# Matmuls without a use in TensorE's waits of the ramp, and seven of batch 1's last fills loaded ahead

## Chip, cores and metric

The kernel runs on one core of a Trainium2 chip. The metric is the device time of the launch in microseconds; the profile's times are microseconds from the first instruction of the program.

## The reference, cut to what matters

```python
xn = layernorm(x)                                    # x: 2 batches x 1024 rows x 1024
s  = xn @ (W * blockmask).T + bias                   # mask of 32x32 blocks
q  = xn.mean(rows) @ Wq.T                            # one query per batch
coeffs = softmax(q @ keys.T / sqrt(128))             # 8 experts, per batch
g  = silu(xn @ W_org.T + sum_e coeffs[e] * (xn @ down[e]) @ up[e])
out = x + s * g
```

So there are two products of 1024 x 1024 x 1024 for each batch: one with the masked weight (called "s" in the kernel), and one with a weight that is W_org plus the experts' low-rank parts, mixed per batch (called "y"). Then they are multiplied, and x is added.

## The kernel before, in words

**Precision by splitting.** Each factor of a product is split in a high part (a cast to the matmul's fp32r type, done on ScalarE) and a low part (the rest, a subtraction on VectorE). A product is three matmuls for each slice of the inner dimension: high by high, high by low, low by high. In `open_gemm` these are lines 441 to 443; its inner function `part(k0, k1)` issues them for slices k0 to k1.

**The ramp.** The first 60 us are ordered by hand on TensorE, VectorE, ScalarE and GpSimd (`manual_schedule`): these engines follow the written order. Row blocks of x are loaded, normalised and transposed on TensorE (`x_turn`, L200), cast and subtracted out of PSUM (`x_hi` L588, `x_lo` L592), while the mask is summed by blocks (`mask_sum`), spread by eight small matmuls (`mask_apply_mm`, L265) and multiplied into the weight (`w_mul`, L571), which is cast (`w_hi`, L576) and subtracted (`w_lo`, L580). `t0` and `t1` are the `part` functions of the first two output tiles in PSUM, p0 and p1: with the first 256 columns of the weight. `warm_up(n)` (L661) issues n matmuls of 128x512 with ones, whose result nobody reads. They run 13 times at the start (`NWARM`), 8 times after row block 0's transposes (`NWARM2`), twice after the mask's matmuls and four times ahead of t0. The parts that the prediction follows stand in the code in this order: `t0(0, 2)`, `w_lo(0, 2)`, `t0(2, 4)`, `x_hi(1, 0)`, `x_lo(1, 0)`, ..., `t1(0, 2)`, `x_turn(1, 1)`, `t1(2, 4)`, `x_lo(0, 1)`, `x_hi(1, 1)`, statistics of row block 2, a mask sum on ScalarE, `t0(4, 8)`, `x_lo(1, 1)`, `shift_of(2)`, the two halves of row block 2's norm, `t1(4, 7)`, `x_turn(2, 0)`, and so on.

**Batch 0** is then computed tile by tile. Meanwhile VectorE prepares sums and differences of batch 1's normalised input and stores them to memory (`xv`).

**Batch 1** uses a scheme of seven products instead of eight for a block of two by two (`quad`): a unit is one pair of 128 output columns for one of the two weights; it has seven factors of the weight, in `raw` (rows of 4 x 128 values in a partition: rows 0 to 3 are loaded, `unit_sum` makes sums in rows 4 to 6 and in row 2), which `unit_split` (L1082 cast, L1083 subtraction) turns into high and low in the tile `ow`. The seven factors of x are loaded from `xv` by `fill` (L1038 load, L1039 cast, L1040 subtraction) into four tiles `xw[j]`, each with seven pieces m. A fill's load goes through a staging buffer, `xs_pool`, with four buffers. The tiles xw[2] and xw[3] take the places of batch 0's x and of batch 0's masked weight, so their casts can't begin before the last tile of batch 0, `s_tile(7)`, has been computed. `product(u, a, m, ...)` (L1190) multiplies factor a of the weight by piece m.

In `quad`, `after(k)` runs the k-th list of `behind`, and `slot(k)` the k-th list of `ahead`, the preparation of the next unit. For unit 0 `behind` holds fills. The products' order is (0, 0) into pa, (4, 3) into py, (5, 4) into pb, (1, 1) into pa, (2, 5) into pb, (6, 2) into py, (3, 6) into pa. Between them ScalarE copies pa into pb (L1221), takes the snapshots s5 of py and s2 of pb (`snap`, L1197), evacuates pa (`out_tile`) and copies pb into pa (L1251); each copy is ahead of the next product that adds to the same place.

**The last tile of batch 0** is evacuated by `flush()` (VectorE L458 and L488), x is added to it by an accumulating transfer of GpSimd (L491), and it is stored by GpSimd (L506). Only then are the pools of batch 0 closed (`late_cms`), in whose place unit 1's `ow` is opened.

Outside of the ramp a scheduler places the instructions, with the written order as its priority; in the trace VectorE and ScalarE follow the written order.

Of the kernel before, what the change touches and what calls it, by code (L numbers as in the profile page):

```python
# [25 lines left out]
E_, R_, KQ = 8, 64, 128  # L26
EPS = 1e-5
NWARM = 13
NWARM2 = 8


@with_exitstack
def kernel(
# [94 lines left out]
    raw = natp.tile([P, 7, 4, P], F32, name="raw")  # L128
# [142 lines left out]
    def mask_apply_cp(qr):  # L271
        nc.vector.tensor_copy(m_sb[:, :, 8 * qr : 8 * (qr + 1)], spread[qr])
# [158 lines left out]
    def open_gemm(b, i, w, c0=0, n=NH):  # L431

        ps = ps_acc.tile([P, NH], F32, name="acc_ps", tag="acc_ps")[:, :n]
        g, j = divmod(i, 4)
        xs = xg[(b, g)]
        cols = slice(j * P, (j + 1) * P)
        wc = slice(c0, c0 + n)

        def part(k0, k1):
            for kt in range(k0, k1):  # L440
                nc.tensor.matmul(ps, lhsT=xs[:, kt, 0, cols], rhs=w[:, kt, 0, wc], start=kt == 0, stop=False)  # L441
                nc.tensor.matmul(ps, lhsT=xs[:, kt, 0, cols], rhs=w[:, kt, 1, wc], start=False, stop=False)  # L442
                nc.tensor.matmul(ps, lhsT=xs[:, kt, 1, cols], rhs=w[:, kt, 0, wc], start=False, stop=kt == NKT - 1)  # L443

        return ps, part
# [94 lines left out]
    J = lambda f, *a: (lambda: f(*a))  # L540
# [43 lines left out]
    def x_turn(i, h):  # L584
        turn((i, h), lambda k: xr[i][:, (4 * h + k) * P : (4 * h + k + 1) * P])

    def x_hi(i, h):
        nc.scalar.copy(g0[:, 4 * h : 4 * h + 4, 0, i * P : (i + 1) * P], turned[(i, h)])  # L588
# [7 lines left out]
    def x_stats(i, h):  # L596
        bn(i, xr[i], h)
# [41 lines left out]
    with tc.manual_schedule(engines={mybir.EngineType.PE, mybir.EngineType.DVE, mybir.EngineType.Activation, mybir.EngineType.Pool}):  # L639
# [19 lines left out]
        def warm_up(n):  # L659
            for _ in range(n):  # L660
                nc.tensor.matmul(  # L661
                    warm, lhsT=ones_r, rhs=ones_r.unsqueeze(1).to_broadcast([P, 4, P]), start=True, stop=True
                )
# [9 lines left out]
        x_turn(0, 1)  # L673
        warm_up(NWARM2)
        x_stats(1, 0)
# [7 lines left out]
        mask_spread(0)  # L683
        shift_of(1)
        mask_apply_mm(0)
        warm_up(2)
        mask_apply_cp(0)
        x_hi(0, 1)
        x_norm_half(1, 0)
# [10 lines left out]
        w_hi(0, 2)  # L700
        p0, t0 = open_gemm(0, 0, s0, 0, NQ)
        p1, t1 = open_gemm(0, 1, s0, 0, NQ)
        t0(0, 2)
        w_lo(0, 2)
        t0(2, 4)
        x_hi(1, 0)
        x_lo(1, 0)
        w_mul(0, 4, nc.gpsimd)
# [316 lines left out]
        xw = {}  # L1025
        XV = (0, 2, 3, 4, 5, 1, 6)

        def fill(j, m, pool=None):

            if j not in xw:  # L1030
                home, tag = ((wpool, "w"), (xpool, "xg"), (xpool, "xg"), (wpool, "w"))[j]
                xw[j] = home.tile([P, 7, 2, NH], F32R, name="xw", tag=tag)
            if pool is None:
                st = misc[:, len(spare) % 3, :]
                spare.append(m)
            else:
                st = pool.tile([P, NH], F32, name="xs")
            nc.sync.dma_start(st, xv[j, :, XV[m], :])  # L1038
            nc.scalar.copy(xw[j][:, m, 0, :], st)  # L1039
            nc.vector.tensor_tensor(xw[j][:, m, 1, :], st, xw[j][:, m, 0, :].bitcast(F32), ALU.subtract)  # L1040

        spare = []
        ORDER_X = (0, 3, 4, 1, 5, 2, 6)
# [86 lines left out]
        cm_xs, xs_pool = open_pool("xs", 4, side="right")  # L1130
# [48 lines left out]
        def res_load(u, i, t):  # L1179
            if u == len(units) - 1:  # L1180
                n = units[u][1] + 4 * i
                res = pools_b1["tmp"].tile([P, NH], F32, name="rest", tag="rest", bufs=3)
                nc.sync.dma_start(res, xT[n * P : (n + 1) * P, S + t * NH : S + (t + 1) * NH])
                held[(i, t)] = res
# [15 lines left out]
        def quad(u, ahead, behind=()):  # L1200

            def after(k):
                for job in behind[k : k + 1]:
                    for f in job:
                        f()

            def slot(k):
                for job in ahead[k]:
                    job()

            pa = ps_acc.tile([P, NH], F32, name="acc_ps", tag="acc_ps")
            if u == 0:
                py = ps_s.tile([P, NH], F32, name="py", tag="ps_s")
                product(u, 0, 0, pa, True, (0, 1))
                product(u, 4, 3, py, True, (0, 1))
                product(u, 0, 0, pa, True, (2, 3))
            else:
                product(u, 0, 0, pa, True)
            after(0)
            pb = ps_acc.tile([P, NH], F32, name="acc_ps", tag="acc_ps")  # L1220
            nc.scalar.copy(pb, pa)  # L1221
            slot(0)
            if u == 0:
                product(u, 4, 3, py, True, (2, 3))
            else:
                py = ps_s.tile([P, NH], F32, name="py", tag="ps_s")
                product(u, 4, 3, py, True)
            after(1)
            s5 = snap(py, "s5")
            res_load(u, 0, 0)  # L1230
            slot(1)
            product(u, 5, 4, pb, False)
            after(2)
            s2 = snap(pb, "s2")
            nc.vector.tensor_tensor(py, py, s2, ALU.add)
            res_load(u, 0, 1)
            slot(2)
            product(u, 1, 1, pa, False)
            after(3)
            out_tile(u, 0, 0, pa)  # L1240
            res_load(u, 1, 1)
            slot(3)
            product(u, 2, 5, pb, False)
            after(4)
            if u == len(units) - 1:
                halves = [(c, ps_acc.tile([P, NH], F32, name="acc_ps", tag="acc_ps")[:, :NQ])
                          for c in (slice(0, NQ), slice(NQ, NH))]
                for c, pc in halves:
                    nc.scalar.copy(pc, pb[:, c])
            else:  # L1250
                nc.scalar.copy(pa, pb)  # L1251
            nc.vector.tensor_tensor(pb, pb, s5, ALU.add)
            slot(4)
            if u == len(units) - 1:
                out_tile(u, 1, 1, pb)
                res_load(u, 1, 0)
                product(u, 6, 2, py, False)
                out_tile(u, 0, 1, py)
                for c, pc in halves:
                    product(u, 3, 6, pc, False, cols=c)  # L1260
                    out_tile(u, 1, 0, pc, c)
                return
            product(u, 6, 2, py, False)
            out_tile(u, 0, 1, py)
            out_tile(u, 1, 1, pb)
            slot(5)
            product(u, 3, 6, pa, False)
            out_tile(u, 1, 0, pa)
            slot(6)

        for m in ORDER_X[:2]:
            for j in (2, 3):
                fill(j, m, xs_pool)
        flush()
        store_out(0, nc.gpsimd)
        close(*[cm for cm, _ in late_cms])
# [1 line left out]
        cm_g, pools_b1["gate"] = open_pool("gate", 4)  # L1278
        cm_t2, pools_b1["tmp2"] = open_pool("tmp2", 1)
        ahead = unit_jobs(1)  # L1280
        behind = [[J(fill, j, m, xs_pool) for j in (2, 3)] for m in ORDER_X[2:]]
        quad(0, ahead, behind)
        close(cm_xs)
        cm_t, pools_b1["tmp"] = open_pool("tmp", 1, side="right")
# [59 lines left out]
```

## Time and profile before

| what | us |
|---|---|
| median of three runs | 456.31 |
| lowest and highest | 455.27, 458.14 |
| profiled execution | 457.36 |
| its span, first to last instruction | 455.6 |
| TensorE busy in the span | 442.5 |
| VectorE busy | 289.1 |
| ScalarE busy | 177.4 |
| mean granted TensorE clock | 0.991 |

A line of the order of time gives start and length in us, the engine, the source line, the operation, what it writes and reads, the shapes and the count; in brackets stands how long the engine had been idle before, and what ended that. The granted clock is the share of TensorE's full clock that the chip allowed.

### The profile page before, as it was taken

The numbers are of one execution on the slowest core, as the hardware profiler recorded it, in microseconds if no ns is written. First come the engines' busy times: TensorE is split into PE (matmuls) and PEld (weight loads), VectorE is DVE, ScalarE is ACT, GpSimd is POOL, SyncE is SP. The second block draws the span as 40 slices with busy tenths as digits, with TensorE's granted clock in tenths as the row PEclk, the third lists the DMA queues.
The fourth block names the chain that finished last, engine by engine and source line by source line (L and its number), as shares of the span: only waits on it lengthen the run. The fifth ranks groups of instructions, "written<-read, shape, count | busy, mean of one in ns | idle before, by whom it ended". The sixth has DMA issues, their size and how long they took to land.

```text
span 455.6 us, 5779 instructions
## 1 busy us (share of the span) xinstructions
PE 442.5 (97%) x2059; PEld 365.6 (80%) x2059; DVE 289.1 (63%) x474; ACT 177.4 (39%) x294; POOL 74.9 (16%) x90
## 2 busy tenths in 40 slices
PE   7799999999999999999999999989999999999996
PEld 5689888788878888888887888867888888888885
DVE  6879787763558568766457667459465295455625
ACT  4566715655622222225233135148243432431520
POOL 3755310001211302231000000110020020002000
PEclk9799999999999999999999999999999999999999
DMA  8993505787974968797879897674274247208103
GB/s 276 391 367 128 178 24 168 258 268 220 268 241 102 299 202 285 252 351 242 272 219 319 226 307 207 191 236 139 87 155 126 88 99 179 92 12 212 55 1 115
DMA packets 47421, 89.52 MB, mean 196 GB/s; under 512 B 4768, under 2 KB 15264, under 8 KB 47392
## 3 DMA queue, kind: packets, MB, share of 16 engines
q1 hardware_dynamic: 30624, 66.08, 43.3%
q0 software_dynamic: 6304, 15.21, 14.6%
q10 hardware_dynamic: 10464, 7.87, 5.4%
q8 instruction: 16, 0.26, 0.2%
q14 instruction: 13, 0.11, 0.1%
HBM read 69.21 MB, written 19.92 MB: 196 GB/s over the span
## 4 chain that ended last, share of the span: by engine, by line
PE 81%; DVE 7%; DMA 5%; issue 3%; ACT 3%; SPq 0%; DVEq 0%; ACTq 0%
PE acc_ps L1190 22%; PE acc_ps L443 11%; PE acc_ps L441 11%; PE acc_ps L442 11%; PE py L1190 9%; PE psw L407 5%; PE psw L405 5%; PE psw L406 5%; DMA xs<-xv 2%; DMA raw<-in_x_dram 1%; DVE slot L580 1%; DMA misc<-in_up_dram 1%; DMA ds<-in_down_dram 1%; DVE ramp L571 1%; DVE wo L412 1%
## 5 line engine op out<-in xcount | busy, mean ns | idle before, releaser
L1190 PE MATMUL acc_ps<-xw,ow 128*128 128x512 f32 (+1 forms) x492 | 113.6, 387 | 2.6 <-ACT s L1197 2.2
L442 PE MATMUL acc_ps<-slot,xgrp 128*128 128x512 f32 (+1 forms) x288 | 106.8, 371 | 2.7 <-DVE slot L580 2.7
L1190 PEld LDWEIGHTS acc_ps<-xw,ow 128*128 128x128 f32 x492 | 90.9, 188 | 22.9 <-ACT s L1197 2.6
L441 PE MATMUL acc_ps<-slot,xgrp 128*128 128x512 f32 (+1 forms) x288 | 107.6, 374 | 0.1
L443 PE MATMUL acc_ps<-slot,xgrp 128*128 128x512 f32 (+1 forms) x288 | 106.7, 371 | 0.7 <-DVE xgrp L592 0.7
L442 PEld LDWEIGHTS acc_ps<-slot,xgrp 128*128 128x128 f32 x288 | 55.4, 192 | 12.2 <-DVE slot L580 3.6
L443 PEld LDWEIGHTS acc_ps<-slot,xgrp 128*128 128x128 f32 x288 | 55.3, 192 | 10.1 <-DVE xgrp L592 1.1
L441 PEld LDWEIGHTS acc_ps<-slot,xgrp 128*128 128x128 f32 x288 | 55.4, 192 | 9.1 <-DVE stash L455 0.3
L407 PE MATMUL psw<-cut,dlo 128*128 128x512 f32 x128 | 50.1, 392 | 0.2 <-DVE dlo L397 0.2
L405 PE MATMUL psw<-cut,dhi 128*128 128x512 f32 x128 | 50.0, 390 | 0.1
L406 PE MATMUL psw<-cut,dhi 128*128 128x512 f32 x128 | 49.8, 389 | 0.0
L1190 PE MATMUL py<-xw,ow 128*128 128x512 f32 x192 | 46.9, 392 | 0.0
L1190 PEld LDWEIGHTS py<-xw,ow 128*128 128x128 f32 x192 | 36.1, 188 | 8.0
L1083 DVE TENSOR_TENSOR ow<-raw,ow 128x1024 fp32r<-128x1024 f32 (+1 forms) x32 | 34.5, 1088 | 10.4 <-ACT ow L1082 10.4
L491 POOL DMA_DIRECT2D stash<-in_x_dram x16 | 14.4, 899 | 133.4 <-DVE stash L488 133.4
L396 ACT CAST dhi<-ds 128x512 fp32r<-128x512 f32 x32 | 19.7, 615 | 40.6 <-DMA ds<-in_down_dram 16.5
L412 DVE TENSOR_TENSOR wo<-wo,psw 128x512 f32<-128x512 f32 x32 | 21.9, 685 | 17.5 <-PE psw L407 17.3
L397 DVE TENSOR_TENSOR dlo<-ds,dhi 128x512 fp32r<-128x512 f32 x32 | 22.0, 687 | 12.9 <-ACT dhi L396 12.8
L1082 ACT CAST ow<-raw 128x1024 fp32r<-128x1024 f32 (+1 forms) x32 | 29.4, 940 | 1.6 <-DVE wo L412 1.6
L407 PEld LDWEIGHTS psw<-cut,dlo 128*128 128x128 f32 x128 | 24.0, 188 | 6.0 <-DVE dlo L397 1.1
L405 PEld LDWEIGHTS psw<-cut,dhi 128*128 128x128 f32 x128 | 24.0, 188 | 5.4 <-ACT dhi L396 0.5
L406 PEld LDWEIGHTS psw<-cut,dhi 128*128 128x128 f32 x128 | 24.1, 188 | 5.1
(174 smaller groups left out, 468.7 us busy)
## 6 DMA issues: line engine op xcount, KB each, us to landing
ds<-in_down_dram SPq DMA_DIRECT2D x32, 256.0 KB, 3.8
wo<-in_worgT_dram SPq DMA_DIRECT2D x32, 256.0 KB, 4.0
raw<-in_x_dram SPq DMA_DIRECT2D x11, 512.0 KB, 5.8
stash<-in_x_dram POOLq DMA_DIRECT2D x16, 256.0 KB, 4.7
raw<-in_wu_dram SPq DMA_DIRECT2D x8, 512.0 KB, 4.9
yu<-wo ACTq DMA_DIRECT2D x16, 256.0 KB, 4.6
xs<-xv SPq DMA_DIRECT2D x16, 256.0 KB, 3.9
raw<-yu SPq DMA_DIRECT2D x8, 512.0 KB, 3.7
```

Source lines behind the costliest of these rows:

```text
L396: nc.scalar.copy(dhi, ds)
L397: nc.vector.tensor_tensor(dlo, ds, dhi.bitcast(F32), ALU.subtract)
L405: nc.tensor.matmul(ps, lhsT=dhi[:, c, :], rhs=u[c][:, 0, :], start=c == 0, stop=False)
L406: nc.tensor.matmul(ps, lhsT=dhi[:, c, :], rhs=u[c][:, 1, :], start=False, stop=False)
L407: nc.tensor.matmul(ps, lhsT=dlo[:, c, :], rhs=u[c][:, 0, :], start=False, stop=c == 3)
L412: nc.vector.tensor_tensor(ws, ws, ps, ALU.add)
L441: nc.tensor.matmul(ps, lhsT=xs[:, kt, 0, cols], rhs=w[:, kt, 0, wc], start=kt == 0, stop=False)
L442: nc.tensor.matmul(ps, lhsT=xs[:, kt, 0, cols], rhs=w[:, kt, 1, wc], start=False, stop=False)
L443: nc.tensor.matmul(ps, lhsT=xs[:, kt, 1, cols], rhs=w[:, kt, 0, wc], start=False, stop=kt == NKT - 1)
L1082: nc.scalar.copy(o[:, a:b, 0], raw[:, a:b])
L1083: nc.vector.tensor_tensor(o[:, a:b, 1], raw[:, a:b], o[:, a:b, 0].bitcast(F32), ALU.subtract)
L1190: nc.tensor.matmul(ps, lhsT=o[:, a, wl, j, :], rhs=xw[j][:, m, xl, cols], start=start and j == 0 and k == 0, stop=j == 3 and k == 2, skip_ ...
```

## The change

In the ramp: NWARM2 goes from 8 to 12; three matmuls without a use in place of two follow the mask's; and `part` gets an argument `between`, a function that it calls after the first of a slice's three matmuls. For t0's slices 0 to 3 it issues 3, 2, 4 and 0 such matmuls.

In batch 1: seven fills of xw[2] and xw[3] in place of four stand ahead of unit 0's `quad`; the fifth to seventh of them load into rows 4 to 6 of `raw` in place of the staging pool (argument `at`). The other seven are spread over `behind` as 2, 2, 2, 1, where there were five lists of two. And in `quad` each `after(k)` moves behind the copy, the snapshot or the evacuation that had stood after it. Its last call, `after(4)`, goes.

```diff
-NWARM2 = 8
+NWARM2 = 12
...
-        def part(k0, k1):
+        def part(k0, k1, between=None):
             for kt in range(k0, k1):
                 nc.tensor.matmul(ps, lhsT=xs[:, kt, 0, cols], rhs=w[:, kt, 0, wc], start=kt == 0, stop=False)
+                if between:
+                    between(kt)
                 nc.tensor.matmul(ps, lhsT=xs[:, kt, 0, cols], rhs=w[:, kt, 1, wc], start=False, stop=False)
...
         mask_apply_mm(0)
-        warm_up(2)
+        warm_up(3)
...
-        t0(0, 2)
+
+        keep_busy = lambda kt: warm_up((3, 2, 4, 0)[kt])
+        t0(0, 2, keep_busy)
         w_lo(0, 2)
-        t0(2, 4)
+        t0(2, 4, keep_busy)
...
-        def fill(j, m, pool=None):
+        def fill(j, m, pool=None, at=None):
...
-            if pool is None:
+            if at is not None:
+                st = at
+            elif pool is None:
                 st = misc[:, len(spare) % 3, :]
...
-            after(0)
             pb = ps_acc.tile([P, NH], F32, name="acc_ps", tag="acc_ps")
             nc.scalar.copy(pb, pa)
+            after(0)
             slot(0)
...
-            after(1)
             s5 = snap(py, "s5")
             res_load(u, 0, 0)
+            after(1)
             slot(1)
             product(u, 5, 4, pb, False)
-            after(2)
             s2 = snap(pb, "s2")
             nc.vector.tensor_tensor(py, py, s2, ALU.add)
             res_load(u, 0, 1)
+            after(2)
             slot(2)
             product(u, 1, 1, pa, False)
-            after(3)
             out_tile(u, 0, 0, pa)
             res_load(u, 1, 1)
+            after(3)
             slot(3)
             product(u, 2, 5, pb, False)
-            after(4)
...
-        for m in ORDER_X[:2]:
-            for j in (2, 3):
-                fill(j, m, xs_pool)
+
+        todo = [(j, m) for m in ORDER_X for j in (2, 3)]
+        for k in range(7):
+            fill(*todo.pop(0), xs_pool, raw[:, k].rearrange("p j n -> p (j n)") if k > 3 else None)
...
-        behind = [[J(fill, j, m, xs_pool) for j in (2, 3)] for m in ORDER_X[2:]]
+        behind = [[J(fill, *todo.pop(0), xs_pool) for _ in range(n)] for n in (2, 2, 2, 1)]
```

ORDER_X is (0, 3, 4, 1, 5, 2, 6); so the seven fills ahead are both tiles' pieces 0, 3 and 4, and xw[2]'s piece 1.

## Prediction

> **What bounds the kernel now.** I read the share of each engine first, then TensorE's idle places by stage (busy time by stretch), then the order of time on TensorE and ScalarE at those places, and the chain that ended last.
>
> ```profile
> span 455.6 us, 5779 instructions
> PE 442.5 (97%) x2059; PEld 365.6 (80%) x2059; DVE 289.1 (63%) x474; ACT 177.4 (39%) x294; POOL 74.9 (16%) x90
> ...
> PE 81%; DVE 7%; DMA 5%; issue 3%; ACT 3%; SPq 0%; DVEq 0%; ACTq 0%
> ```
>
> TensorE is busy for 97%; so only 13.1 us of idle time, and slow time inside the busy time, can be won. By stretch (columns: length, PE, PEld, DVE, ACT, POOL busy with counts, granted clock, DMA share, GB/s):
>
> ```profile
> 11.39:17.82 6.43, 3.84 (x25) 2.55 (x24) 6.09 (x10) 4.38 (x8) 5.69 (x5) 0.93 1.04 393
> 17.82:23.75 5.93, 5.92 (x27) 5.93 (x28) 4.41 (x10) 2.32 (x5) 4.00 (x3) 0.50 1.06 392
> ...
> 94.00:198.00 104.00, 103.67 (x484) 85.64 (x482) 69.08 (x120) 35.06 (x61) 21.51 (x34) 1.00 0.78 238
> 198.00:240.00 42.00, 42.00 (x188) 34.78 (x187) 23.76 (x42) 14.55 (x24) 3.54 (x4) 1.00 0.85 272
> ...
> 294.00:314.00 20.00, 17.39 (x75) 13.46 (x74) 13.39 (x21) 12.54 (x21) 2.04 (x3) 1.00 0.57 179
> 314.00:449.00 135.00, 135.00 (x591) 110.72 (x590) 73.01 (x91) 48.98 (x74) 10.52 (x12) 1.00 0.38 103
> ```
>
> Two places stand out: 17.82 to 23.75, where TensorE is busy all the time at half the clock, and 294 to 314, where it idles 2.6 us. Between and after them it has almost no slack, so what is won at either place is carried to the end. The three waits ahead of the first place, in TensorE's order of time:
>
> ```profile
> 14.94 0.39 PE L442 MATMUL acc_ps<-slot,xgrp 128*128 128x256 f32 x1 [0.83 <-DVE slot L580]
> 16.13 0.38 PE L442 MATMUL acc_ps<-slot,xgrp 128*128 128x256 f32 x1 [0.57 <-DVE slot L580]
> 17.82 0.58 PE L442 MATMUL acc_ps<-slot,xgrp 128*128 128x256 f32 x1 [1.07 <-DVE slot L580]
> 18.20 0.41 PE L443 MATMUL acc_ps<-slot,xgrp 128*128 128x256 f32 x1
> ```
>
> After 18.20 the matmuls start 0.213 us apart; from 24.01 on 0.119 us. The second place, on ScalarE and TensorE:
>
> ```profile
> 307.14 0.62 ACT L1039 CAST xw<-xs 128x512 fp32r<-128x512 f32 x1 [0.50 <-DMA xs<-xv]
> 307.67 0.58 ACT L1197 COPY s<-acc_ps 128x512 f32<-128x512 f32 x1
> ...
> 308.30 3.06 PE L1190 MATMUL acc_ps<-xw,ow 128*128 128x512 f32 x12 [2.19 <-ACT s L1197]
> ```
>
> The copy s2 could run when the product before the last was done (about 303.2), but two fills stand ahead of it on ScalarE, and these wait for their transfers.
>
> [...] the clock falls at 16.92 and returns at 23.75, two windows of 3.41. Stretches of that length give PE busy 2.40 of 3.41 (10.10 to 13.51, clock kept), 1.84 (13.51 to 16.92, clock then falls), 2.47 and 2.17 (303.64 to 310.47, kept). [...] here three gaps of 0.83, 0.57 and 1.07 did it, so the measurement decides: at 64% busy and more the clock stayed, at 54% it fell. [...]
>
> **The ramp, step by step.** Four matmuls are added to the eight before the mask's (NWARM2), one after the mask's, and nine (3, 2, 4) into the three waits. Eight took 2.09 us, so one step is (2.09 - 0.39)/7 = 0.243. Twelve from 8.41 issue until 11.32; the mask's matmul waits for VectorE until 11.39 anyway. Three instead of two from 11.65 issue until 12.38; the transposes wait for ScalarE's half row until 12.37. Three in the first wait: 13.96 to 14.69, under 14.94. Two in the second: 15.40 to 15.89, under 16.13. Four in the third: 16.60 to 17.57, under 17.82. So they cost nothing, VectorE's subtractions (L580, 3.48 us for three) being the cover; without it each costs 0.24. Each window is then over 85% busy, and the clock stays full.
>
> Then I follow the written order from 17.82 with full-clock steps (0.119 a matmul, 0.35 for four transposes). t0's last five and t1's first six issue until 19.24; x_turn(1,1) ends at 19.84 instead of 21.39; x_hi(1,1) on ScalarE starts at 19.87 instead of 21.43, then the mask sum, and row block 2's norm at 21.45 instead of 22.96 (VectorE's shift is ready at 21.40). On TensorE t1(2,4), t0(4,8), t1(4,7) are 27 matmuls, ending at 22.92 with x_lo(1,1) done at 21.28; x_turn(2,0) starts there instead of at 25.56: 2.64 us earlier. x_hi(2,0) follows 2.64 earlier (23.55 for 26.19), x_lo(2,0) too (24.17 for 26.81; GpSimd's pow for block 3, behind the sum that ends at 23.6, is done at 24.18, before shift_of(3) at 24.8). What was late next, x_lo for t2, then x_turn(3,0), mask, w_mul on VectorE at 30.96, statistics, means, hangs on that chain. The loads don't hold it: the last wT part landed at 21.15, xlate at 27.56, the xT tiles at 29.65 to 33.18, and their users come at 28.3, 32 and 37.9. Afterwards the loads wait for buffers, which come earlier too. **Ramp: 2.64 us**; ends: 0 (the gain is swallowed by a chain that I haven't seen between 60 and 94, where VectorE and ScalarE run close to TensorE) and 2.9 (all of TensorE's own slow time: 26 steps of 0.093, the transposes 0.36, the first 0.16).
>
> **The fills, step by step.** Batch 1's last two weight tiles (j = 2, 3) have 14 fills; each is a load, a cast (621 ns, 0.55 apart) and a subtraction (686 ns, 0.61 apart). Before, four were loaded ahead of the last projection tile's end (294.1) and ten later; now seven, three of them in rows 4 to 6 of raw, free once unit 0's splits are done (284.3) and needed again only by unit 1's sums, which VectorE does after the seven subtractions. SP issues these three about 286, so they land long before 294.
>
> ScalarE: seven casts from 294.30 end at 298.15; the copy into pb, whose product ends at 298.45, runs to 299.1 (before 300.21). TensorE goes on at 299.69 instead of 300.27. Fills 8 and 9 follow, s5, fills 10 and 11, whose loads leave at 295.67 to 297.48 as before; s2 runs at 302.6 to 303.2, ahead of fill 12. TensorE's product into pb starts unhindered at 299.69 + 24 x 0.227 = 305.14, instead of 308.30. That removes both waits, 3.1 us in start times.
>
> What is late next: the seven subtractions stand ahead of the last tile's evacuation on VectorE, so it ends 1.86 us later (3 x 0.61), the accumulating transfer starts at 301.1 instead of 299.24, and with the 9.83 us of before (6.57, its release, 2.86) the last store lands at 310.9 instead of 309.07. The weights of unit 1 (ow, opened over the stash's place) wait for it. On ScalarE behind that wait stand the cast (1.04), and the copy of pb into pa, which TensorE needs. Fills 12 to 14 leave at 301.3 to 302.5 and land at about 307.4 to 308.4 (5.6 to 6.6 us beside the accumulation before), so ScalarE reaches the wait at about 309.8. Cast 310.95, copy 311.9 to 312.5, product at 312.55. TensorE would be there at 310.59, so 1.96 are given back; before it was there at 313.99. **Fills: 1.44 us**; ends: -3.7 (rival D) and 3.1.
>
> **Sum.** The profiled execution took 457.36 (span 455.6 and 1.76 around it): 457.36 - 2.64 - 1.44 = 453.3. The three shown runs have the median 456.31 (455.27 to 458.14); a window that falls now for two lengths, now for one or none, would spread them by that much, so against the median I expect 3.0, or 0.7%.
>
> **Rivals.** B: the store doesn't hold the copy (the transfers collide less, or the evacuation goes first): 457.36 - 2.64 - 3.1 = 451.6. For it: the other accumulations landed in 3.6 to 5.3 us; against: ScalarE's own row leads to 309.8 anyhow. C: the ramp's gain is lost between 60 and 94 or the clock falls still: 457.36 - 1.44 = 455.9. For it: the chain runs through VectorE, ScalarE and loads there; against: that chain itself begins in the ramp. D, slower: the last tile's evacuation is ordered behind eleven subtractions and the sum of s2 (304.4), its accumulation leaves at 306.2, the store lands at 316.0, and ScalarE's copy comes at 317.6: 3.7 later than before, and with a ramp that brings 0 to 2.64 it gives 458.4 (with the ramp) to 461.1. It decides from a landing later than about 315. Against it: in the trace VectorE kept the written order.
>
> **Numbers.** A 0.52, B 0.24, C 0.14, D 0.10. Predicted: 453.3. The range takes B at its low end with 0.5 for the loads' scatter and C, and leaves half of D out: 451.1 to 457.0. About 1% (4.6 us) is what a measurement can tell from no change. Faster by more needs under 451.75: most of B and a little of A, 0.27. Slower by more needs over 460.9: the worse part of D and what I haven't thought of, 0.07. Within: 0.66.
>
> **What would show it.** Right: granted clock 1.0 from 17 to 24, matmuls 0.119 apart there, x_turn(2,0) near 22.9, TensorE 2.6 earlier at 94 and at 294; s2 right behind its product; a new wait of some 2 us on the copy of pb into pa, behind the store. Wrong: a granted clock of 0.5 in the ramp, later starts of the mask's matmul, or no wait at the copy (B).

## The result, and the profile after

Five runs of the changed kernel have the median 451.53 us (451.14 to 452.98); five of the kernel before beside them 456.59 (455.27 to 458.14). The ratio is 0.9895, interval 0.9865 to 0.9924. The profiled execution took 451.53 against 457.36, so 5.83 less from profile to profile and 5.06 less in the medians. The forecast was 453.3, which meant 4.06 less from profile to profile and 3.0 less in the medians; rival B's figure was 451.6.

The head of the profile page of the changed kernel, its TensorE line, and the shares of the chain that ended last:

```profile
span 449.8 us, 5809 instructions
PE 441.3 (98%) x2073; PEld 364.9 (81%) x2073; DVE 289.3 (64%) x474; ACT 177.8 (40%) x294; POOL 74.8 (17%) x90
...
PE 90%; DVE 5%; ACT 1%; DMA 1%; issue 1%; SPq 0%; DVEq 0%; ACTq 0%
```

TensorE has 14 more counted matmul records, yet it is busy for 1.2 us less: the useful matmuls of the ramp run at full clock now. Its idle time goes from 13.1 to 8.5 us. By stretch, with the same columns as before; the last line is unit 0's stretch, 3 us earlier than before's because the whole schedule is:

```profile
11.39:17.82 6.43, 6.15 (x37) 4.19 (x35) 6.05 (x10) 4.51 (x9) 5.46 (x5) 1.00 1.04 391
17.82:23.75 5.93, 5.77 (x49) 5.69 (x49) 5.31 (x13) 3.16 (x5) 4.18 (x3) 1.00 1.05 391
291.00:311.00 20.00, 20.00 (x88) 16.06 (x87) 15.54 (x24) 13.65 (x23) 2.04 (x3) 1.00 0.66 187
```

In the same 5.93 us 49 matmuls stand where there were 27, and the clock column reads 1.00 for 0.50. In unit 0's stretch TensorE has no idle time at all; before it idled for 2.6 us there. TensorE's order of time in the ramp shows the new matmuls filling the waits:

```profile
14.19 0.85 PE L663 MATMUL warm<-ones_r 128*128 128x512 f32 x3
15.17 0.39 PE L444 MATMUL acc_ps<-slot,xgrp 128*128 128x256 f32 x1
...
16.83 1.07 PE L663 MATMUL warm<-ones_r 128*128 128x512 f32 x4
18.06 0.39 PE L444 MATMUL acc_ps<-slot,xgrp 128*128 128x256 f32 x1 [0.16 <-DVE slot L582]
18.28 0.28 PE L445 MATMUL acc_ps<-slot,xgrp 128*128 128x256 f32 x1
18.40 0.27 PE L441 MATMUL acc_ps<-slot,xgrp 128*128 128x256 f32 x1
```

The matmuls behind 18.28 start 0.12 apart. The bracket of 0.16 at 18.06 shows that VectorE still ends last: the four matmuls ahead of it cost nothing. In unit 0, on ScalarE:

```profile
299.96 0.59 ACT L1203 COPY s<-acc_ps 128x512 f32<-128x512 f32 x1 [0.59 <-PE acc_ps L1196]
301.68 0.62 ACT L1045 CAST xw<-xs 128x512 fp32r<-128x512 f32 x1 [1.13 <-DMA xs<-xv]
304.20 0.62 ACT L1045 CAST xw<-xs 128x512 fp32r<-128x512 f32 x1 [1.90 <-DMA xs<-xv]
...
306.50 1.05 ACT L1088 CAST ow<-raw 128x1024 fp32r<-128x1024 f32 x1 [0.36 <-DMA out_dram<-stash]
307.45 0.58 ACT L1256 COPY acc_ps<-acc_ps 128x512 f32<-128x512 f32 x1
```

and on TensorE:

```profile
296.97 8.53 PE L1196 MATMUL acc_ps<-xw,ow 128*128 128x512 f32 x36
305.33 2.95 PE L1196 MATMUL py<-xw,ow 128*128 128x512 f32 x12
308.12 5.78 PE L1196 MATMUL acc_ps<-xw,ow 128*128 128x512 f32 x24
```

The snapshot s2 (299.96) now waits for its own product, not for a load; the fills that wait for loads stand behind it, where TensorE does not need ScalarE. TensorE runs 36 matmuls through what had been two waits. The wait for the last store is there, but it is 0.36 and not 2: the copy of pb into pa ends at 308.03, and TensorE comes to it at 308.1.

How the 5.87 us at that point add up:

| at | before | after | gained by then |
|---|---|---|---|
| `x_turn(2, 0)` | 25.56 | 23.13 | 2.43 |
| first matmul for batch 0's expert weights (`psw`, L405) | 71.06 | 68.66 | 2.40 |
| unit 0's first product | 294.10 | 291.39 | 2.71 |
| product (5, 4) into pb, after unit 0's first | +6.17 | +5.58 | 3.30 |
| product (2, 5) into pb, after unit 0's first | +14.20 | +11.15 | 5.76 |
| product (3, 6) into pa, after unit 0's first | +19.89 | +16.73 | 5.87 |

Thus, of the profiles' difference, 2.71 had come by unit 0's first product and 3.16 came in unit 0. The ramp itself is best counted from the first transposes, which began at 7.29 and at 7.51: from there to the first `psw` matmul it takes 63.77 before and 61.15 after, 2.62 less. The 0.31 between 71 us and unit 0 is not the ramp's; that stretch differs by as much between other runs.

### The profile page after: what moved, and what is told of

It is laid out like the page before. It is cut to its first block, busy times and chain, and to the rows that moved or that the text cites. A ratio compares the mean times of both kernels' runs of the same rounds, so it can differ in the third digit from the quotient of the medians.

```text
span 449.8 us, 5809 instructions
## 1 busy us (share of the span) xinstructions
PE 441.3 (98%) x2073; PEld 364.9 (81%) x2073; DVE 289.3 (64%) x474; ACT 177.8 (40%) x294; POOL 74.8 (17%) x90
## 4 chain that ended last, share of the span: by engine, by line
PE 90%; DVE 5%; ACT 1%; DMA 1%; issue 1%; SPq 0%; DVEq 0%; ACTq 0%
PE acc_ps L1196 25%; PE acc_ps L441 13%; PE acc_ps L445 12%; PE acc_ps L444 12%; PE py L1196 10%; PE psw L407 6%; PE psw L405 6%; PE psw L406 6%; DMA raw<-in_x_dram 1%; DVE slot L582 1%; DVE ramp L573 1%; DVE st L144 1%; DVE wo L412 1%; DVE xgrp L594 0%; ACT raw L178 0%
## 5 line engine op out<-in xcount | busy, mean ns | idle before, releaser
L444 PE MATMUL acc_ps<-slot,xgrp 128*128 128x512 f32 (+1 forms) x288 | 105.7, 367 | 0.6 <-DVE slot L582 0.4
L444 PEld LDWEIGHTS acc_ps<-slot,xgrp 128*128 128x128 f32 x288 | 54.3, 189 | 10.6 <-DVE slot L582 2.1
L445 PEld LDWEIGHTS acc_ps<-slot,xgrp 128*128 128x128 f32 x288 | 54.2, 188 | 10.2 <-DVE xgrp L594 1.1
L441 PEld LDWEIGHTS acc_ps<-slot,xgrp 128*128 128x128 f32 x288 | 54.3, 188 | 9.1 <-DVE stash L457 0.3
L405 PE MATMUL psw<-cut,dhi 128*128 128x512 f32 x128 | 49.9, 390 | 0.2 <-DVE wo L412 0.2
L405 PEld LDWEIGHTS psw<-cut,dhi 128*128 128x128 f32 x128 | 24.0, 188 | 5.5 <-ACT dhi L396 0.5
L1179 POOL DMA_DIRECT2D gate<-in_xT_dram x12 | 10.5, 905 | 94.4 <-DVE gate L1173 68.9
```

What stands on the lines that cost most here:

```text
L405: nc.tensor.matmul(ps, lhsT=dhi[:, c, :], rhs=u[c][:, 0, :], start=c == 0, stop=False)
```

## The experiments

The edits are relative to the changed kernel, but for the first, which is the kernel before with one part of the change. Each ratio is against runs of the kernel before on the same chip.

### The ramp's part alone (`ramp_only`) and the fills' part alone (`fills_only`)

`ramp_only` is the kernel before with NWARM2 = 12, `warm_up(3)` and the nine in t0's waits. `fills_only` takes these out of the changed kernel:

```diff
-NWARM2 = 12
+NWARM2 = 8
...
-        warm_up(3)
+        warm_up(2)
...
-        keep_busy = lambda kt: warm_up((3, 2, 4, 0)[kt])
+        keep_busy = lambda kt: warm_up((0, 0, 0, 0)[kt])
```

> The kernel before with the ramp's part of the change alone. Theory (two separate gains that add up): the granted clock stays at 1.0 from 17 to 24 us, the ramp is 2.7 us shorter, the waits of 0.42 and 2.19 us in unit 0 stay: 456.6 - 2.7 = 453.9. Rival 1 (in many runs of the kernel before the clock doesn't fall, or falls for one window only): the profile shows 2.7, the medians only 1.2 to 1.9, 454.7 to 455.4. Rival 2 (the two parts need each other, since TensorE arrives earlier at the fills): nearly nothing, 456.

> The changed kernel with the ramp as before (NWARM2 8, two after the mask, none in t0's waits). Theory: the clock falls in the ramp as before, mean clock 0.991, and the two waits in unit 0 go: 456.6 - 3.2 = 453.4. Rival 1: its runs scatter in granted clock between 0.991 and 0.998, [...] and the time goes with the clock: some 2.7 us between the runs with the lowest and the highest clock. Rival 2: under 1 us gained.

`ramp_only`: median 455.68 of 11 runs against 457.47, ratio 0.9965 (0.994 to 0.9991); the 1.79 between the medians are rival 1's (1.2 to 1.9) and not the theory's 2.7. Its profiled run took 454.86, 2.50 under the profiled kernel before. `fills_only`: 453.6 of 6 runs, ratio 0.9916 (0.9888 to 0.9943). The ratios multiply to 0.988; the two parts together measured 0.9895. The ramp's part leaves unit 0's waits where they were, on TensorE in its order of time:

```profile
298.18 5.85 PE L1193 MATMUL acc_ps<-xw,ow 128*128 128x512 f32 x24 [0.40 <-ACT acc_ps L1224]
305.84 0.50 PE L1193 MATMUL acc_ps<-xw,ow 128*128 128x512 f32 x1 [1.81 <-ACT s L1200]
```

In `fills_only` unit 0 is that of the changed kernel (product (2, 5) 11.15 after the first), and the clock falls in the ramp, by stretch:

```profile
15.01:18.42 3.41, 1.29 (x7) 0.83 (x6) 3.41 (x4) 3.09 (x6) 3.41 (x4) 1.00 1.06 377
18.42:21.84 3.42, 2.80 (x13) 2.81 (x14) 3.32 (x7) 0.00 (x0) 1.70 (x2) 0.50 1.06 387
21.84:25.25 3.41, 3.41 (x18) 3.41 (x17) 1.99 (x4) 2.61 (x5) 2.91 (x2) 0.50 1.03 412
```

This was the slowest of the six runs: its clock was also at half from 8.18 to 11.60, so for 3.42 us more. So each part does its own work. That the ramp's part is worth 2.5 from profile to profile and only 1.8 in the medians has its reason in the clock of the single runs, at the end of this section.

### Which of the added matmuls (`nine_only`, `no_nine`, `nine_doubled`)

`nine_only` takes out the four and the one (NWARM2 = 8, `warm_up(2)`); `no_nine` keeps these and takes out the nine:

```diff
-        keep_busy = lambda kt: warm_up((3, 2, 4, 0)[kt])
+        keep_busy = lambda kt: warm_up((0, 0, 0, 0)[kt])
```

> The changed kernel without the matmuls added ahead of t0 (NWARM2 8, two after the mask's); the nine in t0's waits stay. Theory: the nine alone hold the clock, since the three waits at 14 to 17.8 us were the ones that let the window fall to 54% busy: as the changed kernel, 451.5. Rival: the wait of 0.95 us ahead of the mask's matmuls counts too, and the clock falls for one or two windows in some runs: 452.5 to 454.2.

> The changed kernel without the nine matmuls in t0's waits; NWARM2 12 and three after the mask's stay. Theory: the clock falls as before, mean clock 0.991, 451.5 + 2.7 = 454.2, as fills_only. Rival: the five added ahead are enough to hold the clock: 451.5.

`nine_only`: 451.74, ratio 0.9872 (0.9843 to 0.9901), mean clock 0.999 to 1.0 in each of its 6 runs. The nine suffice; the other five do nothing that shows. `no_nine`: 453.44, ratio 0.9913 (0.9884 to 0.9942), about as `fills_only`. In 5 of its 6 runs the mean clock is 0.995 to 0.996 and not the 0.991 that was expected: one stretch of 3.41 us at half clock in place of two, an estimate from the mean (3.41 us at half clock take 0.0037 off the mean of a span of 455.6). Its profile is of the sixth, where the clock did not fall though the waits of 0.82, 0.57 and 1.07 stood there as before:

```profile
12.97:16.38 3.41, 2.02 (x12) 1.37 (x10) 3.41 (x5) 2.75 (x6) 3.41 (x4) 1.00 1.02 404
16.38:19.79 3.41, 2.34 (x20) 2.14 (x19) 3.41 (x5) 0.43 (x2) 2.43 (x2) 1.00 1.09 365
```

The edges of these windows come from the record of the clock. In before it turned at 16.95, 23.78 and 453.86, so 6.827 and 430.079 us apart, which are 2 and 126 times 3.413; in the changed kernel one stretch of 443.733 at full clock, 130 times 3.413, ends at 448.32. Such a length of 3.413 is called a window in this document. In `no_nine` the edges are counted back in this length from the turn at 449.88, an estimate. Here the edge at 16.38 cuts the waits into two windows, 59% and 69% busy; in `fills_only` the one from 15.01 to 18.42, behind which the clock fell, was 38% busy. So with the waits of before's ramp the clock stayed in one run, and in another it was at half for 6.83 us (18.42 to 25.25); what decided it is not shown.

This profile also shows what the nine matmuls are worth when the clock stays: nothing. From the first transposes (7.12) to the first `psw` matmul (68.26) `no_nine` takes 61.14, where the changed kernel takes 61.15 and before 63.77. The ramp's 2.62 are the clock's, and holding it costs TensorE nothing.

```diff
-        keep_busy = lambda kt: warm_up((3, 2, 4, 0)[kt])
+        keep_busy = lambda kt: warm_up((6, 4, 8, 0)[kt])
```

> The changed kernel with 6, 4 and 8 matmuls without a use in t0's three waits in place of 3, 2 and 4. Theory (VectorE's subtractions cover just the nine; each more costs its 0.24 us of TensorE's time, and the ramp's chain runs through TensorE): t0's third slice starts 1.45 us later, and 1.2 to 1.5 of it reach the end: 453.0. Rival (the ramp's end is set by VectorE, ScalarE and the loads, and TensorE has slack there): 451.6 to 452.

`nine_doubled`: 452.93, ratio 0.992 (0.9892 to 0.9947). Twice as many reach beyond the waits. On TensorE:

```profile
17.04 1.99 PE L663 MATMUL warm<-ones_r 128*128 128x512 f32 x8
18.86 0.28 PE L444 MATMUL acc_ps<-slot,xgrp 128*128 128x256 f32 x1
```

L444 comes right behind the eighth, with no wait, at 18.86 for 18.06; counted from t0's first matmul (13.92 for 14.08) it is 0.96 later, where 1.45 had been expected. Eight took 1.99, so a step is (1.99 - 0.39)/7 = 0.229 and not the 0.243 read from the eight at 8.41. The profiled runs differ by 1.45 (452.98 for 451.53), but from the first transposes to the first `psw` matmul it is 0.87 more (62.02 for 61.15). The trace thus shows that the nine matmuls are free and that eighteen are not, and their price is under the expected one; the medians agree in direction, but the interval overlaps with the changed kernel's.

### Loads ahead, or order on ScalarE (`order_only`, `ahead_only`)

`order_only` keeps the new order (copies and snapshots ahead of the fills), and loads only four ahead, so that ten stand in `behind`:

```diff
-        for k in range(7):
-            fill(*todo.pop(0), xs_pool, raw[:, k].rearrange("p j n -> p (j n)") if k > 3 else None)
+        for k in range(4):
+            fill(*todo.pop(0), xs_pool)
...
-        behind = [[J(fill, *todo.pop(0), xs_pool) for _ in range(n)] for n in (2, 2, 2, 1)]
+        behind = [[J(fill, *todo.pop(0), xs_pool) for _ in range(n)] for n in (2, 2, 2, 2, 2)]
...
+            after(4)
             slot(4)
```

`ahead_only` keeps the seven loads and puts each `after(k)` back where it was:

```diff
+            after(0)
             pb = ps_acc.tile([P, NH], F32, name="acc_ps", tag="acc_ps")
             nc.scalar.copy(pb, pa)
-            after(0)
             slot(0)
...
+            after(2)
             s2 = snap(pb, "s2")
...
-            after(2)
             slot(2)
```

> The changed kernel with four fills ahead, all through the staging pool, and ten behind in five lists of two as before; only the places of after(k) are the new ones. Theory (both halves of the fill part are needed): s2 runs right behind its product, but fills 9 and 10, which the product after it reads, are still loaded late (landing some 12 us after the last projection tile's end), so TensorE waits some 1.2 us inside that product: 451.6 + 1.2 = 452.8. Rival 1 (the order on ScalarE does it all): 451.6. Rival 2 (the loads do it all): both waits stay, 451.6 + 3.1 = 454.7.

> The changed kernel with the seven fills ahead, and each after(k) back at its old place, ahead of the copy or snapshot. Theory (both halves are needed): the copy into pb stands behind fills 8 and 9, whose loads land 4.4 and 5.0 us after the last projection tile's end, so the wait of some 0.5 us stays; s2 stands behind fills 12 and 13, landing 10 to 12 us after that end, for another 1 to 1.5: 451.6 + 1.8 = 453.4. Rival 1 (the order does it all): 454.7. Rival 2 (the loads do it all): 451.6.

`order_only`: 453.05, ratio 0.9929 (0.9904 to 0.9954), where 452.8 was expected. `ahead_only`: 455.27 of 22 runs, ratio 0.9964 (0.9948 to 0.9981), no better than the ramp's part alone; 453.4 was expected and even rival 1 (454.7) was under it. In `ahead_only` ScalarE takes s2 behind a fill whose load came late, and TensorE waits for s2, first ScalarE, then TensorE:

```profile
303.87 0.62 ACT L1045 CAST xw<-xs 128x512 fp32r<-128x512 f32 x1 [1.68 <-DMA xs<-xv]
304.40 0.58 ACT L1203 COPY s<-acc_ps 128x512 f32<-128x512 f32 x1
```

```profile
297.44 5.85 PE L1196 MATMUL acc_ps<-xw,ow 128*128 128x512 f32 x24 [0.36 <-ACT acc_ps L1227]
305.03 1.20 PE L1196 MATMUL acc_ps<-xw,ow 128*128 128x512 f32 x4 [1.74 <-ACT s L1203]
```

These are the two waits of before, 0.36 and 1.74. In `order_only` both are gone, and another stands at another place, within product (6, 2), for a fill's subtraction:

```profile
306.66 1.79 PE L1196 MATMUL py<-xw,ow 128*128 128x512 f32 x7
309.19 0.50 PE L1196 MATMUL py<-xw,ow 128*128 128x512 f32 x1 [0.74 <-DVE xw L1046]
```

It had been expected in product (2, 5); the place was wrong, the size (product (3, 6) 1.0 later than in the changed kernel, 1.2 expected) about right. Of the 3.16 in unit 0 the order alone brings 2.15 (17.74 for 19.89), the loads ahead alone some 0.5 (19.38), and the rest needs both. Each figure is from one profile: against `ramp_only`, which has the same ramp and where product (3, 6) starts 19.50 after unit 0's first, the order alone brings 1.76, the loads alone 0.12, and both 2.77. `order_only` has another wait of 1.2 at 248, of which more below.

### What the last store can cost (`late_store`, `evac_first`)

`late_store` puts a second accumulating transfer ahead of the last tile's store, so that x is added to that tile twice:

```diff
         nc.gpsimd.dma_start(res, x[at], accum_op=ALU.add)
+        if kind == "s" and h == 1 and i == 7:
+            nc.gpsimd.dma_start(res, x[at], accum_op=ALU.add)
```

> The changed kernel, in which x is added twice to the last tile of batch 0 (one more accumulating transfer of GpSimd after the first), so that its store comes some 5 us later; that tile's output is s*g + 2x. Theory (what the prediction called the give-back: ScalarE's cast into unit 1's weights waits for that store, since they lie in its place, and the copy of pb into pa stands behind it): the store lands some 5 us later, TensorE waits 4.5 to 5 us at the product after the copy, and the clock falls after so long a wait, for up to 2.7 more: 456.2 to 459. Rival (the store doesn't hold ScalarE, which is why nothing was given back): 451.6.

`late_store`: 460.97, ratio 1.0097 (1.0064 to 1.013), slower than the 456.2 to 459 that were expected. The store lands at 313.11, 6.8 later than in the changed kernel and not some 5, and on ScalarE, then on TensorE:

```profile
313.28 1.04 ACT L1090 CAST ow<-raw 128x1024 fp32r<-128x1024 f32 x1 [7.74 <-DMA out_dram<-stash]
314.24 0.58 ACT L1258 COPY acc_ps<-acc_ps 128x512 f32<-128x512 f32 x1
```

```profile
314.87 1.65 PE L1198 MATMUL acc_ps<-xw,ow 128*128 128x512 f32 x3 [6.41 <-ACT acc_ps L1258]
```

That is the chain of the prediction, store to cast to copy to TensorE, and the side on which rival D lay. It costs more than its wait: product (3, 6) starts 6.58 later than in the changed kernel, and the profiled run ends 8.93 later (460.46 for 451.53). By stretch:

```profile
308.50:312.80 4.30, 0.00 (x0) 0.00 (x0) 0.00 (x0) 0.00 (x0) 0.00 (x0) 1.00 0.80 191
312.80:319.63 6.83, 4.76 (x11) 3.84 (x12) 4.18 (x4) 4.60 (x6) 0.00 (x0) 0.50 0.23 79
319.63:330.00 10.37, 10.37 (x47) 8.53 (x47) 1.77 (x3) 2.94 (x5) 0.00 (x0) 1.00 0.15 51
```

TensorE's 11 matmuls in 312.80 to 319.63 run at half clock. That stretch is two windows long, and begins 2.07 ahead of the end of TensorE's wait (314.87). What took TensorE 4.76 us at half clock would take some 2.4 at full clock (an estimate from the busy time and the granted clock); that accounts for the other 2.3.

`evac_first` evacuates the last tile ahead of the seven fills on VectorE, and was run beside the changed kernel once more (`after_again`):

```diff
+        flush()
         todo = [(j, m) for m in ORDER_X for j in (2, 3)]
```

> The changed kernel once more, as the measure for the kernels beside it: 451.5, granted clock 0.996 to 1.0 in each run.

> The changed kernel with the last projection tile's evacuation written ahead of the seven fills. Theory (in the changed kernel the store of that tile lands about when ScalarE comes to the cast that waits for it, 306.3 for 306.1, so it costs TensorE 0 to 0.2 us): the store lands 1.9 us earlier, ScalarE's copy of pb into pa comes no more than 0.4 us earlier, and TensorE gains 0 to 0.2: 451.4. Rival (the delay of the store costs, as the prediction had it): 1 us or more gained, 450.5.

`after_again`: 452.45, ratio 0.9908 (0.9882 to 0.9935). `evac_first`: 451.98, ratio 0.9893 (0.987 to 0.9917). The evacuation passes all seven subtractions, not only the three that the change had added: the accumulating transfer leaves at 294.38 for 299.35, 4.97 earlier. The store behind it takes 1.1 longer (3.5 for 2.3) and lands at 303.29 for 307.18. First `after_again`, then `evac_first`, on ScalarE:

```profile
307.36 1.05 ACT L1088 CAST ow<-raw 128x1024 fp32r<-128x1024 f32 x1 [0.39 <-DMA out_dram<-stash]
308.32 0.57 ACT L1256 COPY acc_ps<-acc_ps 128x512 f32<-128x512 f32 x1
```

```profile
306.90 1.04 ACT L1088 CAST ow<-raw 128x1024 fp32r<-128x1024 f32 x1
307.85 0.58 ACT L1256 COPY acc_ps<-acc_ps 128x512 f32<-128x512 f32 x1
```

ScalarE's wait is gone and the copy is 0.47 earlier, but product (3, 6) starts 16.74 after unit 0's first in both: TensorE had not been waiting. The medians' 0.47 is within the scatter. In two other profiles with the new order and the seven loads ahead TensorE did wait a little for this copy: 0.35 in `no_nine`, 0.18 in `nine_doubled`. So the store costs TensorE between nothing and 0.35 in these executions, not 1.96.

### Does the wait in unit 0 cost a clock window too (`ahead_busy`)?

`ahead_only`, with seven matmuls nobody reads ahead of product (2, 5) in unit 0:

```diff
+            if u == 0:
+                idle_ps = ps_w.tile([P, NH], F32, name="idle_ps", tag="psw")
+                for _ in range(7):
+                    nc.tensor.matmul(idle_ps, lhsT=ow[u][:, 5, 0, 0, :], rhs=xw[0][:, 4, 0, :], start=True, stop=True)
             product(u, 2, 5, pb, False)
```

> The kernel ahead_only (seven fills ahead, old places of after(k), 455.27) with seven matmuls without a use ahead of the product that waits some 1.7 us for s2; their result goes nowhere. Theory (that wait lets the clock fall in those runs [...] nine of 22 runs with 0.994 to 0.996): the wait is as long as before, but no run has a mean clock under 0.998 other than by the end of the run, and the median is that of the runs of ahead_only with 0.999 and more, 454.6. Rival (the low clocks come from the end of the run or from the ramp): a third or more of the runs at 0.994 to 0.996 as before, 455.3.

`ahead_busy`: 455.27 of 20 runs, ratio 0.9954 (0.9939 to 0.997). The wait is filled:

```profile
303.75 1.79 PE L1252 MATMUL idle_ps<-xw,ow 128*128 128x512 f32 x7
305.66 1.20 PE L1196 MATMUL acc_ps<-xw,ow 128*128 128x512 f32 x4
```

In `ahead_only` the mean clock was 0.994 to 0.996 in 9 of 22 runs (mean 456.48; the other 13, at 0.999 and more, 454.69). With the seven matmuls it was so in 1 of 20 (0.996). And `order_only`, which has no such wait and ran on the same chip as `ahead_only`, was at 0.999 to 1.0 in each of its 7 runs. So with the wait of 1.74 us in unit 0 the mean clock was lower in about two runs of five, with the wait filled in one of twenty, and in `ahead_only` the runs with the lower clock are 1.8 slower: shown. A lower median was expected, 454.6, and didn't come; the 19 runs at full clock have a mean of 455.18, 0.5 above those of `ahead_only`. The two kernels ran on different chips, and as ratios to the kernel before beside them they are 0.9954 and 0.9964, with intervals that overlap. In the one profile of each, `ahead_busy` has a wait of 0.50 at 248 us (see the next heading) that `ahead_only` hasn't, while unit 0 takes as long (product (3, 6) starts 19.45 after its first product, for 19.38). Whether chip or wait is the 0.5 stays open.

### A version with both late places eased (`both`)

`evac_first`, with one fill of batch 0's last third moved from tile 2 to tile 3, since the trace showed a new wait at 248 us (TensorE for a subtraction that stands behind a fill on VectorE):

```diff
-                if i < 3 and (i == 2 or k in (1, 2)):
+                if (i < 3 and k in (1, 2)) or (i == 3 and k == 0):
                     fills(0, 1)
```

> evac_first, and the fill of xw[0] that stands in the fold after the second load of the experts' weights moved to the first fold of the next tile. Theory (TensorE, earlier now, waits there at about 248 us for a subtraction on VectorE behind that fill's, and the fill waits for its load: 0 to 1.2 us in the traces so far): no wait over 0.2 us there, and the median 0.3 to 0.6 under evac_first, 451.0. Rival (the wait is moved to the next fold): as evac_first, 451.4.

`both`: 451.07, ratio 0.9875 (0.9849 to 0.99). The wait, here in the waits of 246 to 250 us of `after_again`,

```profile
PE psw L407 <- DVE dlo L397: 0.3, 1, 0.3
```

is gone in it, and unit 0's first product stands at 290.74. But the profiles of the changed kernel, `nine_only` and `ahead_only` have no such wait either, without this edit, so one profile doesn't show that the edit removed it. In the median it is below `evac_first` and `after_again`, and clearly below the kernel before; its interval overlaps with those of the first two, so against the changed kernel 1.4 us is a lead but no more.

### The clock of the single runs

Runs of eight kernels by their mean granted clock, count and mean time (us). A window of 3.413 at half clock takes 0.0037 off the mean of a span of 455.6, two take 0.0075 (estimates from these two numbers, by which lost windows are counted in runs without a profile); the cut at 0.998 leaves room for a fall after the last matmul (in the changed kernel's profile from 448.3 to its end at 449.8):

| kernel | 0.998 and more | 0.994 to 0.997 | under 0.994 |
|---|---|---|---|
| before (28 runs beside `ahead_only`) | 3: 454.56 | 9: 456.27 | 16: 457.85 |
| `ramp_only` | 6: 454.60 | 4: 456.53 | 1: 458.30 |
| `ahead_only` | 13: 454.69 | 9: 456.48 | none |
| `fills_only` | 2: 452.84 | 3: 453.71 | 1: 455.25 |
| `no_nine` | 1: 452.37 | 5: 453.77 | none |
| `nine_only` | 6: 451.63 | none | none |
| the changed kernel (the five runs of the result) | 4: 451.61 | 1: 452.98 | none |
| `after_again` (the same kernel) | 6: 452.80 | none | none |

`ramp_only`, `fills_only`, `no_nine` and `nine_only` ran on one chip, before and `ahead_only` on a second, `after_again` on a third; the medians of before on them lie between 457.18 and 457.47. Read along the rows: from one column to the next it is 1.4 to 1.9 more, but for the first step of `fills_only`, with few runs, 0.9. Read down the first column: the changed kernel alone is at 451.61 and at 452.80 in two groups of runs, so this column can't tell differences of 1 us. Within that, the ramp's part brings nothing at full clock (454.60 for 454.56), and the fills' part brings the rest. That `fills_only` and `no_nine` lie some 1 us over `nine_only` at full clock, on the same chip but in only three runs, stays open; in the traces the ramp is as fast without the nine when the clock stays (61.14 for 61.15 above). The profiled run of before was one with two windows lost (at 0.50 from 16.95 to 23.78, mean clock 0.991); by their mean clock others lost one or none, which is why the medians differ by less than the profiles.

## Why the prediction was right or wrong

The direction, and the two gains, were right; the forecast was 1.8 too high, by one term, the give-back. In the medians 3.0 less was forecast and 5.06 came.

- **The ramp, right.** 2.64 was forecast. `x_turn(2, 0)` came at 23.13 and not near 22.9, because the first transposes, which stand ahead of everything that was added, began 0.22 later in this execution (7.51 for 7.29); counted from them it is 2.65 earlier. That 2.71 stand at unit 0 is this gain less the late start, and 0.31 that came between 71 us and unit 0, which the prediction did not have: so close a match there is luck. The clock stayed at 1.0, the steps fell to 0.12, the nine were hidden by VectorE. A step of the added matmuls was 0.229 and not 0.243; nothing hung on it.
- **Of the ramp's matmuls** four and one were not needed (`nine_only`), and "Each window is then over 85% busy" came true: in the three windows from 7.99 to 18.23, counted back from the clock's turn at 448.32, TensorE was busy for 3.36, 3.36 and 3.02 of 3.41 us, so for 89% to 99%.
- **The waits in unit 0, right.** 3.1 in start times was forecast for both, and 3.16 came. The prediction's own sums give 3.40 at product (3, 6) if nothing is given back (313.99 less 310.59), so rival B should have read 451.3; its step of 0.227 was too short there, since the 24 matmuls ahead took 5.58 and not 5.45. The product into pb, forecast at 305.14, came at 302.54, which is 305.25 with the ramp's 2.71 put back. The order on ScalarE alone does about two thirds of it: 2.15 of 3.16 (`order_only`).
- **The give-back, wrong: the step that failed** is "with the 9.83 us of before (6.57, its release, 2.86) the last store lands at 310.9". The accumulating transfer started at 298.49, which is 301.20 with 2.71 put back, where 301.1 was forecast. But it took 5.11 and not 6.57, and the store 2.33 and not 2.86; with the 0.40 between them 7.83. It landed at 306.32, or 309.03 in the prediction's clock. The fills beside it landed at 301.66, 304.18 and 305.49 (304.4 to 308.2 in that clock, for 307.4 to 308.4), so that ScalarE came to the wait at 308.85 for 309.8, the store landed some 0.2 later, and the copy ended at 310.74, just when TensorE came (310.8). GpSimd's lines, first before, then after:

```profile
299.24 0.89 POOL L491 DMA_DIRECT2D stash<-in_x_dram  x1 [7.64 <-DVE stash L488]
306.21 0.58 POOL L506 DMA_DIRECT2D out_dram<-stash  x1 [5.50 <-DMA stash<-in_x_dram]
```

```profile
298.49 0.89 POOL L493 DMA_DIRECT2D stash<-in_x_dram  x1 [9.60 <-DVE stash L490]
304.00 0.58 POOL L508 DMA_DIRECT2D out_dram<-stash  x1 [4.04 <-DMA stash<-in_x_dram]
```

Both terms had been taken over from the old schedule to the new one, and they go with the schedule more than with chance. With the old order and four loads ahead the accumulating transfer took 6.57 and 6.16 (before, `ramp_only`) and the store 2.87 in both. With seven loads ahead and nothing else changed around that store, in eight profiles, the accumulating transfer took 5.06 to 5.11, once 5.63 (`nine_doubled`), and the store 2.33 or 2.34. In `order_only`, with the new order and four loads ahead, they took 4.67 and 3.56. Which of the transfers beside them makes the difference is not shown. Rival B named this term; its "3.6 to 5.3" are the four accumulations ahead of the last one, while all of before's sixteen lie between 3.6 and 8.8. Product (3, 6), forecast at 312.55 in that clock, came at 310.83: these 1.72 are the miss of 1.8.

- **It was close.** `late_store` shows that the chain is as drawn, and that the slack was nearly none: counted from unit 0's first product the store landed 6.6 later there, and product (3, 6) started 6.6 later.
- **Rival C, in part.** In the profile the ramp's gain went through. In the medians it is less than 2.64, since not each run of before lost two windows (16 of 28 had a mean clock under 0.994); "against the median I expect 3.0", the author's estimate, had this right in kind: the medians took 0.8 off the profiles' difference, 1.0 was forecast.
- **Rival D** did not come; where `late_store` brought it about, with a landing at 313.11 (315.65 in the prediction's clock, just past its 315), the kernel was slower than before, profiled by 3.1 and in the medians by 1%. Counting the wait alone, as the prediction did, misses the 6.83 us at half clock that came with it.
- **"At 64% busy and more the clock stayed, at 54% it fell" does not hold as a rule.** By the records it fell at 53% (before, with the window put at 13.54 to 16.95, where the record of the clock has it) and 38% (`fills_only`), and stayed at 59% (`no_nine`) and, in this window of `ahead_only`, at 49%:

```profile
302.23:305.65 3.42, 1.68 (x8) 1.06 (x7) 1.81 (x3) 1.58 (x3) 0.58 (x1) 1.00 0.86 306
```

So TensorE's busy share by these records doesn't tell whether the clock falls. They are no exact measure: a record of a 256-column matmul lasts 0.28 for a step of 0.12, so a scattered one counts more than one in a row. The edges in `ahead_only` are counted back in windows of 3.413 from the clock's turn at 452.41, an estimate too. Nor do the gaps alone tell it: with 0.83, 0.57 and 1.07 in the ramp the clock fell in before's profile, and with 0.82, 0.57 and 1.07 it stayed in that of `no_nine`; with 1.74 in unit 0 it stayed in the profile of `ahead_only`, of whose 22 runs 9 had the lower mean clock.

What stays open: what decides whether the clock falls, where before's lost windows lie in the runs that were not profiled (ramp or unit 0), which transfers sped up the last store, and the half microsecond of `ahead_busy`.

## What to carry to other kernels

Here waits of 0.57 to 1.07 us on TensorE in the ramp, and one of 1.74 in unit 0, came with a lower mean clock (0.994 to 0.996 for 0.998 and more), in 5 of the 6 runs of `no_nine` and 9 of the 22 of `ahead_only`, and with the waits filled in none of the 6 of `nine_only` and 1 of the 20 of `ahead_busy`. Fill such a wait with matmuls that end before the wait does, count in the profile what covers them, and look at the clock of many runs, not of one profile. On an engine that follows the written order, as ScalarE did in these traces (s2 at 307.67, behind the casts of 306.03 and 307.14), put the instruction that TensorE waits for ahead of those that wait for a load: here that order alone brought 1.8 to 2.2 us, the loads ahead alone 0.1 to 0.5, and both together more than the sum. And a transfer's time belongs to the schedule it was read in: here it repeated within 0.6 us in eight profiles with the new schedule, and was 1.5 under the time of the old one. If a forecast hangs on such a time, take it as an end of a range, and weigh the case in which it lands early as heavily.

## What the runs showed of the hardware

- The stretches between the clock's turns at 16.95, 23.78 and 453.86 in before's profile were 6.827 and 430.079 us long, 2 and 126 times 3.413, and the one to 448.32 in the changed kernel's 443.733, 130 times. By the mean clock (0.998 and more, 0.994 to 0.997, under 0.994) the runs of one kernel, with no change of code, fall in three groups (means of 454.6, 456.3 and 457.9 for 28 runs of before).
- A wait of 6.4 us came with a run 8.9 longer (`late_store`): the clock was at half for 6.83 us, from 2.07 before the wait's end.
- TensorE's busy share of 3.41 us, by the records, didn't decide the fall: the clock fell after 53% (before) and 38% (`fills_only`), and stayed after 49% (`ahead_only`), 59% (`no_nine`) and 64% (before, 307.05 to 310.47).
- The same store of the last tile took 2.3, 2.9, 3.5 and 5.5 us from issue to landing (the changed kernel, before, `evac_first`, `late_store`), and the accumulating transfer ahead of it 5.1, 6.6, 5.1 and 4.7.
- A wait at 248 us, for a subtraction behind a fill whose load came late, varies from execution to execution: none in five of the fourteen profiles (the changed kernel's among them), 0.2 to 1.2 in the others, 0.2 in before.
